# Expert blocks of a mixture of experts: rows loaded from a register address and turned on VectorE

## The chip, the cores and the metric

The kernel runs on one core of a Trainium2 chip. The metric is the device time of one execution in microseconds (us); a kernel's time is the median over several executions. All data are 32-bit floats.

## What is computed

The input is 8 images of 256 channels and 32 x 32 places, so 8 x 1024 tokens of width 256. Layer 0 is an attention with 8 heads, with its softmax over the queries, and a residual. Layer 1 is an attention without heads on the normalised tokens, a residual, a second normalisation, and a mixture of 8 experts of which each token uses two. The part that matters here is the mixture:

```python
logits = tokens @ router_w.T
probs = softmax(logits)
rw, re = top_k(probs, 2)
rw = rw / rw.sum(-1)
out = tokens
for e in range(8):
    h = gelu(tokens @ w1[e] + b1[e])
    y = h @ w2[e] + b2[e]
    out = out + combine[:, e:e+1] * y      # combine holds rw at re, else 0
```

w1 and w2 are 256 x 256 for each expert.

## The kernel before

The images are worked through one after the other. For each of the first seven, layer 0 (lines 437 to 642) and the attention of layer 1 (`attend`, line 645) run, then the tokens are routed: `dispatch` (line 849) computes for every token its two experts and a place within each expert, and GpSimd scatters the normalised rows into `rows`, a table in DRAM that has 7168 rows for each expert (line 917). The scatters are spread over layer 0 of the next image.

For the eighth image layer 0 runs, and with its products the expert stage `experts` (line 1018) works off the routed rows of the seven images. The rows of an expert are cut into blocks of 256 (`BR`); there are 63 block positions, and `plan` (line 926) computes on the chip which expert each block belongs to (`e_of`), at which row of `rows` it starts, and where its weights lie. It leaves two tables of integers: `row_at`, with one row number for each partition and block, and `w_at`, which points past the end of the table where a buffer already holds the right weights, so that nothing is loaded. After that, attention and a dense form of the experts run for the eighth image, with the results of the seven gathered and stored beside them.

One block goes through these steps:

- `fetch` (line 1024): GpSimd loads the weights of the block's expert from `wpack` into one of four buffers (`wb`, 128 partitions of 1282 values: w1 in two chunks of 128 input features, w2, b1, b2), then with a second indirect load 128 pieces of two neighbouring rows into `xr` (three buffers). TensorE turns them in four transposes of 128 x 128 into PSUM (`px`, line 1044), and VectorE copies them to `xb` (two buffers, line 1046), with features on partitions.
- `hidden` (line 1049): eight products into `ph` (line 1054), and two gelus on ScalarE (line 1064) into `hT`.
- `collect` (line 1073): eight products into `pe` (line 1079), the bias added by VectorE into `yb` (two buffers, line 1088), and a store to `y` from SP's queue (line 1093). A partition holds two neighbouring rows, 2 KB, and the store writes them in one piece.

The loop (line 1100) runs hidden of block b-1, fetch of block b, and collect of block b-2 in one turn. An engine issues its instructions in the order that a scheduler fixes when the program is built: it starts from the program text and moves an instruction ahead where its model sees the engine idle. `issue_after(ins)` holds a group of instructions behind `ins` on the same engine. A buffer's next load waits until its last reader is done: the weights of block b wait for pe and the bias addition of block b-4, which had that buffer.

After block 4 `places` (line 993) runs: for each of the seven images and each of the two choices, five small VectorE operations that turn a token's place within its expert into its row in `y` (`yat`). These are needed when the results are gathered (line 1163).

In layer 0 of every image but the first, SP also relays semaphores: `relay.nop()` (line 551) is an empty instruction on SP that waits for one half of the po products and that the other half waits for.

The squares that the change uses are in the kernel already in two places. `load_squares` and `residual` (lines 417 to 435) load the input so that VectorE's transpose, which turns each square of 32 x 32 for itself, gives the tokens on partitions; and `turn` (line 686) does the same with the attention weights, where 16 moves put the squares in their places.

Of the kernel before, what the change touches and what calls it, by code (L numbers as in the profile page):

```python
# [10 lines left out]
F32 = mybir.dt.float32  # L11
I32 = mybir.dt.int32
AF = mybir.ActivationFunctionType
ALU = mybir.AluOpType
# [5 lines left out]
def kernel(  # L20
# [23 lines left out]
    nc = tc.nc  # L44
    P = 128
    B, C, S = x.shape
    E, D, FF = w1.shape
# [3 lines left out]
    NCC = C // P  # L51
# [3 lines left out]
    NFC = FF // P  # L55
# [3 lines left out]
    WROW = NCC * FF + NFC * D + NFC + D  # L59
    NWB = 3  # L60
    NXB = NWB + 1

    dram = ctx.enter_context(tc.tile_pool(name="dram", bufs=1, space=bass.MemoryType.DRAM))
    const = ctx.enter_context(tc.tile_pool(name="const", bufs=1))
# [10 lines left out]
    def big(name):  # L75

        return ps_big.tile([P, 1024], F32, tag="big", name=name)
# [58 lines left out]
    for e in range(E):  # L136
# [12 lines left out]
    nc.gpsimd.iota(  # L149
        p_iota, [[1, 1]], base=0, channel_multiplier=1, allow_small_or_imprecise_dtypes=True  # L150
    )
    r_iota = const.tile([P, 1], F32, name="r_iota")
    nc.gpsimd.iota(
        r_iota, [[1, 1]], base=0, channel_multiplier=R, allow_small_or_imprecise_dtypes=True
    )
    ones = const.tile([P, P], F32, name="ones")
    nc.gpsimd.memset(ones, 1.0)

# [48 lines left out]


    NB = NT // NH2
    SQ = 32  # L210
    NQ = P // SQ

    def bcast(t, n):

# [66 lines left out]
    def pack():  # L281


        wp = wpack.rearrange("(e p) c -> e p c", p=P)
        for dc in range(NCC):
            nc.sync.dma_start(
                wp[:, :, ts(dc, FF)], w1.rearrange("e (dc p) f -> dc e p f", p=P)[dc]
            )
        at = NCC * FF
        for fc in range(NFC):  # L290
            nc.sync.dma_start(
                wp[:, :, at + fc * D : at + (fc + 1) * D],
                w2.rearrange("e (fc p) d -> fc e p d", p=P)[fc],
            )
# [142 lines left out]
    def layer0(b, xT, begun, routing, xs):  # L437
# [138 lines left out]
        for at in range(last + LAG + 1):  # L576
            g, j = steps[min(at, last)]

            early = at > LAG and j == 1 and (g, j) not in PROJECT
            if at <= last:  # L580
                with tc.issue_after(counted.ins) if counted else nullcontext():
                    score(at, 0, 0)
            if 0 < at <= last + 1:
                with tc.issue_after(counted.ins) if counted else nullcontext():
                    score(at - 1, 1, 1)
                second_max(at - 1, 1)
                soften(at - 1, 1)
            if at >= LAG:
                with tc.issue_after(counted.ins) if counted else nullcontext():
                    gather_values(at - LAG, 0)  # L590
                counted = None
            if at <= last:

                with tc.issue_after(seconds[1].ins) if 1 in seconds else nullcontext():
                    first_max(at, 0)
                score(at, 0, 1)
                score(at, 1, 0)
                second_max(at, 0)
                if not early:
                    soften(at, 0)  # L600
                with tc.issue_after(seconds[0].ins):
                    ahead = divide(at - 1) if at > 0 else seconds[0]
                with tc.issue_after(ahead.ins):
                    first_max(at, 1)
            elif at == last + 1:
                divide(last)
            if at == 0:
                begun.rest()
                share()
            if at >= LAG:  # L610
                array = gather_values(at - LAG, 1)
            if early:
                with tc.issue_after(copied[0].ins), tc.issue_after(copied[1].ins):
                    soften(at, 0)
            if at <= last and (g, j) in PROJECT:
                with tc.issue_after(firsts[at, 1].ins), tc.issue_after(array.ins):
                    share(firsts[at, 1])
                    pair, pq, mm = project_pair(b, xT, g + 1)
                qks.append(pair)
                if (g, j) == PROJECT[-1]:  # L620
                    with tc.issue_after(firsts[at, 1].ins):
                        t1 = residual(b, xs)
                if g == 0:
# [302 lines left out]
    def plan(group):  # L926
# [39 lines left out]
        )  # L966

        base = tmp("p_base", [E])
        nc.vector.tensor_scalar(base, first, -float(BR), r_iota, ALU.mult, ALU.add)
        work = tmp("p_work", [nb, E])  # L970
        lo, hi = tmp("p_lo", [nb]), tmp("p_hi", [nb])
        nc.vector.tensor_mul(work, mine, base.unsqueeze(1).to_broadcast([P, nb, E]))
        nc.vector.tensor_reduce(lo, work, AX.X, ALU.add)
        nc.vector.scalar_tensor_tensor(lo, b_iota[:, :nb], float(BR), lo, ALU.mult, ALU.add)
        nc.vector.tensor_scalar_min(lo, lo, float(cap - R))
        nc.vector.scalar_tensor_tensor(lo, e_of, float(cap), lo, ALU.mult, ALU.add)
        row_at = keep.tile([P, NBMAX], I32, tag="row_at", name=f"row_at_{n}", bufs=2)
        nc.vector.tensor_copy(row_at[:, :nb], lo)
# [14 lines left out]
    def places(group):  # L993

        first = group.first
        for b in group.items:
            gate, kept = group.kept[b]
            ats = []
            for k, (row, exp) in enumerate(kept):
# [13 lines left out]
                at = keep.tile([P, NT], I32, tag=f"yat{k}", name=f"yat{k}_{b}")  # L1013
                nc.vector.tensor_copy(at, to)
                ats.append(at)
            group.kept[b] = gate, ats

    def experts(group):
        n = group.n
        row_at, w_at = group.where  # L1020

        wbs_x = [*wbs, one.tile([P, WROW], F32, tag="v", name="wb_x")]

        def fetch(b):
            wb = wbs_x[b % NXB]
            nc.gpsimd.indirect_dma_start(
                out=wb[:, :],
                out_offset=None,
                in_=wpack[:, :],
                in_offset=bass.IndirectOffsetOnAxis(ap=w_at[:, b : b + 1], axis=0),  # L1030
                bounds_check=E * P - 1,
                oob_is_err=False,
            )
            xr = rowp.tile([P, R, D], F32, tag="xr", name=f"xr_{n}_{b}")
            nc.gpsimd.indirect_dma_start(
                out=xr.rearrange("p r d -> p (r d)"),
                out_offset=None,
                in_=group.rows[:, :],
                in_offset=bass.IndirectOffsetOnAxis(ap=row_at[:, b : b + 1], axis=0),
            )  # L1040
            px = big(f"px_{n}_{b}")
            for dc in range(NCC):
                for r in range(R):
                    nc.tensor.transpose(px[:, ts(dc * R + r, P)], xr[:, r, ts(dc, P)], ident)  # L1044
            xb = two.tile([P, NCC, BR], F32, tag="xb", name=f"xb_{n}_{b}")
            nc.vector.tensor_copy(xb.rearrange("p c t -> p (c t)"), px[:, : NCC * BR])
            return xb

        def hidden(b, xb):
            wb = wbs_x[b % NXB]  # L1050
            ph = big(f"ph_{n}_{b}")
            for fc in range(NFC):
                for dc in range(NCC):
                    nc.tensor.matmul(  # L1054
                        ph[:, ts(fc, BR)],
                        wb[:, dc * FF + fc * P : dc * FF + (fc + 1) * P],
                        xb[:, dc, :],
                        start=(dc == 0),
                        stop=(dc == NCC - 1),
                    )  # L1060
            hT = two.tile([P, NFC, BR], F32, tag=f"qk{b % 2}", name=f"hb_{n}_{b}")
            at = NCC * FF + NFC * D
            for fc in range(NFC):
# [4 lines left out]
                    bias=wb[:, at + fc : at + fc + 1],  # L1068
                    scale=1.0,
                )  # L1070
            return hT

        def collect(b, hT):
            wb = wbs_x[b % NXB]
            py = acc(f"pe_{n}_{b}")
            at = NCC * FF
            for r in range(R):
                for fc in range(NFC):
                    nc.tensor.matmul(  # L1079
                        py[:, ts(r, D)],  # L1080
                        hT[:, fc, ts(r, P)],
                        wb[:, at + fc * D : at + (fc + 1) * D],
                        start=(fc == 0),
                        stop=(fc == NFC - 1),
                    )
            at += NFC * D + NFC
            yb = two.tile([P, R, D], F32, tag="yb", name=f"yb_{n}_{b}")
            added = nc.vector.tensor_add(
# [1 line left out]
                py.rearrange("p (r d) -> p r d", d=D),  # L1090
                wb[:, at : at + D].unsqueeze(1).to_broadcast([P, R, D]),
            )
            nc.sync.dma_start(group.y[ts(b, BR), :].rearrange("(p r) d -> p r d", r=R), yb)
            if b == NXB:
                with tc.issue_after(added.ins):
                    places(group)


        rows, hiddens = {}, {}
        for b in range(group.nb + 2):  # L1100
            if b - 1 in rows:
                hiddens[b - 1] = hidden(b - 1, rows.pop(b - 1))
            if b < group.nb:
                rows[b] = fetch(b)
            if b - 2 in hiddens:
                collect(b - 2, hiddens.pop(b - 2))

    class Results:

# [235 lines left out]
    for b in range(B):  # L1345
# [6 lines left out]
        if b + 1 < B:  # L1352
# [3 lines left out]
            nc.sync.dma_start(groups[0].sums[b], t2)  # L1356
            routing = dispatch(b, n2, l, groups[0])
            continue
        experts(groups[0])
        others = Results(groups[0])  # L1360
        others.begin()
        norm = None
# [54 lines left out]
```

## Time and profile before

| | us |
|---|---|
| median of 3 runs | 2336.58 |
| the runs | 2336.16 to 2338.21 |
| profiled execution, its own time | 2335.55 |
| its span | 2333.5 |
| expert stage: first ph to end of last pe | 1877.51 to 2127.72 |

The granted clock of TensorE in the profiled execution is 0.995 of full speed. Engines that matter in the stage, from the timeline of an ordinary block, and the queues:

| What | Engine | Duration |
|---|---|---|
| ph, eight products | PE | 1.73 us in the chain |
| pe, eight products | PE | 1.73 us in the chain |
| px, four transposes | PE | 0.44 us in the chain |
| xb copy | DVE | median 691 ns |
| yb addition | DVE | median 691 ns |
| gelu, two a block | ACT | median 472 ns each |
| weights, issue of the load | POOL | median 1011 ns |
| rows, issue of the load | POOL | median 953 ns |
| y, issue of the store | SP's queue | median 320 ns |

PE is TensorE, PEld its weight loads, DVE VectorE, ACT ScalarE, POOL GpSimd, SP SyncE; SPq and ACTq are the instructions with which an engine starts a DMA. A name such as `xb<-px` says what an instruction writes and reads. In brackets stands how long the engine had been idle before it and what ended that. The chain of waits is followed back from the last instruction, so a piece in it is what the end waited for. The DMA share is the mean busy share of the core's 16 DMA engines.

### The profile page before, as it was taken

What the parts mean: (1) busy time and instruction counts of PE and PEld (TensorE: products, weight loads), DVE (VectorE), ACT (ScalarE), POOL (GpSimd) and SP (SyncE); (2) the same over time, 40 slices, a digit from 0 to 9 for tenths busy, and PEclk for the clock granted to TensorE, in tenths of its full rate; (3) what the DMA queues carried; (4) which work ended last, traced back from release to release, by engine and by line L of the source; (5) the groups of instructions that cost most, each with busy time, mean ns of one, the idle gap of its engine ahead of it and who ended that gap; (6) DMA issues with size and microseconds to landing.
All of it is one profiled execution on the core that took longest, in us unless ns stands there. A gap on an engine that the chain in (4) does not pass through costs nothing.

```text
span 2333.5 us, 37255 instructions
## 1 busy us (share of the span) xinstructions
PE 2297.1 (98%) x13375; PEld 1255.0 (54%) x13375; DVE 1513.0 (65%) x3660; ACT 1091.7 (47%) x1954; POOL 419.6 (18%) x391
## 2 busy tenths in 40 slices
PE   9999999999999999999999999999999999999898
PEld 3345534563456335633564356435553488887565
DVE  5775578557855785578647774777568763334865
ACT  3663366346634663556355645465545612222411
POOL 0000012000200030003000200020002234444663
PEclk9999999999999999999999999999999999999999
DMA  8995201020103010201020102000110256665664
GB/s 294 385 386 152 66 14 42 9 56 10 46 4 61 6 51 1 46 19 53 3 46 19 49 8 41 23 26 12 26 39 19 83 177 225 222 219 168 183 182 116
DMA packets 219232, 209.23 MB, mean 90 GB/s; under 512 B 120200, under 2 KB 162856, under 8 KB 217256
## 3 DMA queue, kind: packets, MB, share of 16 engines
q1 hardware_dynamic: 192952, 139.13, 19.8%
q0 software_dynamic: 25008, 67.20, 9.3%
q8 instruction: 107, 1.75, 0.3%
q10 hardware_dynamic: 1088, 0.52, 0.1%
q14 instruction: 77, 0.63, 0.1%
HBM read 108.88 MB, written 110.90 MB: 94 GB/s over the span
## 4 chain that ended last, share of the span: by engine, by line
PE 91%; DVE 4%; DMA 2%; issue 1%; ACT 1%; SPq 1%; POOL 0%; DVEq 0%; ACTq 0%; POOLq 0%
PE po L541 19%; PE psc L464 19%; PE ps L672 9%; PE py L713 8%; PE pqk L346 7%; PE pr L638 5%; PE pv L383 4%; PE ph L1054 4%; PE pe L1079 4%; PE pdy L1307 2%; PE pdh L1283 2%; PE px L657 2%; PE pqk L324 2%; PE px L1044 1%; DMA wb<-wpack,w_at 1%
## 5 line engine op out<-in xcount | busy, mean ns | idle before, releaser
L505 ACT ACTIVATE ex<-psc,nmax 128x1024 f32<-128x1024 f32 x512 | 570.1, 1114 | 304.4 <-DVE scrap L488 217.2
L464 PE MATMUL psc<-qk,qk 64*64 64x512 f32 x4096 | 576.9, 593 | 7.8 <-ACT ex L505 7.7
L541 PE MATMUL po<-ex,vs 64*64 64x512 f32 x4096 | 571.2, 592 | 1.2 <-DVE vs L521 0.3
L488 DVE TENSOR_SCALAR_CACHE_REDUCE scrap<-psc,nmax 128x512 f32<-128x512 f32 x512 | 384.3, 751 | 160.8 <-PE psc L464 134.7
L479 DVE TENSOR_REDUCE nmax<-psc 128x1 f32<-128x512 f32 x512 | 350.3, 684 | 9.5 <-PE psc L464 9.5
L464 PEld LDWEIGHTS psc<-qk,qk 64*64 64x64 f32 x4096 | 180.1, 132 | 284.2 <-ACT ex L505 135.8
L541 PEld LDWEIGHTS po<-ex,vs 64*64 64x64 f32 x4096 | 175.9, 132 | 273.7 <-issue 83.6
L713 PE MATMUL py<-n,aT 128*128 128x256 f32 x1024 | 231.4, 379 | 0.2 <-DMA aT<-sq 0.2
L672 PE MATMUL ps<-nT,xa 128*128 128x512 f32 x512 | 228.5, 592 | 0.0
L917 POOL DMA_INDIRECT rows<-n,d_at x112 | 108.8, 972 | 661.2 <-DVE nmax L479 658.4
L713 PEld LDWEIGHTS py<-n,aT 128*128 128x128 f32 x1024 | 193.9, 190 | 50.2 <-issue 23.3
L844 POOL TENSOR_TENSOR t<-t,n 128x2048 f32<-128x2048 f32 x8 | 36.2, 4531 | 874.7 <-DVE n L238 874.7
L697 ACT COPY aT<-sq 32x256 f32<-32x256 f32 x384 | 154.4, 402 | 72.8 <-DVE sq L690 41.3
L346 PE MATMUL pqk<-xT,wqkv 128*128 128x512 f32 x384 | 171.2, 599 | 0.0
L672 PEld LDWEIGHTS ps<-nT,xa 128*128 128x128 f32 x512 | 96.6, 190 | 102.4 <-issue 94.7
L680 DVE TENSOR_REDUCE nmax<-ps 128x1 f32<-128x1024 f32 x64 | 77.9, 1217 | 84.9 <-PE ps L672 84.9
L311 ACT ACTIVATE qk<-pqk,b_qks 128x512 f32<-128x512 f32 x124 | 85.6, 690 | 95.9 <-PE pqk L346 77.1
L346 PEld LDWEIGHTS pqk<-xT,wqkv 128*128 128x128 f32 x384 | 71.0, 190 | 99.9 <-issue 76.8
L383 PE MATMUL pv<-wqkv,xT 128*128 128x512 f32 x256 | 121.9, 605 | 2.1 <-ACT wqkv L106 1.1
L1163 POOL DMA_INDIRECT yk<-y,yat x112 | 110.3, 985 | 69.2 <-issue 26.2
L638 PE MATMUL pr<-wo,res 128*128 128x256 f32 x512 | 111.9, 379 | 0.3 <-ACT res L560 0.3
L1064 ACT ACTIVATE hb<-ph,wb 128x256 f32<-128x256 f32 x96 | 40.2, 470 | 144.8 <-issue 76.7
(191 smaller groups left out, 2441.1 us busy)
## 6 DMA issues: line engine op xcount, KB each, us to landing
rows<-wb SPq DMA_DIRECT2D x7, 8192.0 KB
y<-yb SPq DMA_DIRECT2D x63, 256.0 KB
aT<-sq SPq DMA_DIRECT2D x384, 32.0 KB
xs<-in_x_dram SPq DMA_DIRECT2D x64, 128.0 KB
out_dram<-oT SPq DMA_DIRECT2D x60, 128.0 KB
xT<-in_x_dram SPq DMA_DIRECT2D x7, 1024.0 KB
sums<-t SPq DMA_DIRECT2D x7, 1024.0 KB
o<-sums SPq DMA_DIRECT2D x7, 1024.0 KB
```

The costliest lines, as they stand in the source:

```text
L346: mm = nc.tensor.matmul(pq[:, ts(n, 512)], wqkv[:, cc, t, ts(g, P)], xT[:, cc, ts(n, 512)], start=(cc == 0), stop=(cc == NCC - 1),)
L383: nc.tensor.matmul(pv, self.xT[:, cc, ts(i, P)], wqkv[:, cc, 2, :], start=(cc == 0), stop=(cc == NCC - 1),)
L464: mm = nc.tensor.matmul(pss[at, h][ts(c, DK), ts(n, 512)], k[r, j * P + c * DK : j * P + (c + 1) * DK], q[r, ts(n, 512)], start=True, stop ...
L479: firsts[at, h] = nc.vector.tensor_reduce(nmax, pss[at, h][:, ts(0, 512)], AX.X, ALU.max, negate=True)
L488: seconds[h] = nc.vector.tensor_scalar(scrap, pss[at, h][:, ts(1, 512)], -1.0, nmaxes[at, h], ALU.mult, ALU.min, accum_out=nmax,)
L505: nc.scalar.activation(ex, pss.pop((at, h)), AF.Exp, bias=nmaxes.pop((at, h)), scale=1.0, accum_out=sums[at][:, h : h + 1],)
L541: mm = nc.tensor.matmul(po[n][ts(h, DK), :], vss[at][keys, h, :], exps[at, h][keys, ts(n, 512)], start=(j == 0 and turn == 0), stop=(j == ...
L638: nc.tensor.matmul(pr[:, :C], res[:, g, ts(i, P)], wo[:, g, :], start=(g == 0), stop=(g == NPAIR - 1))
L672: nc.tensor.matmul(psc[:, ts(n, 512)], xa[:, ec, ts(i, P)], nT[:, ec, ts(n, 512)], start=(ec == 0), stop=(ec == NCC - 1),)
L697: move(to[ts(k, SQ), a], since[ts(a, SQ), k])
L713: nc.tensor.matmul(py[:, :D], aT[m], n1[:, m, :], start=(m == 0), stop=(m == NT - 1))
L1163: ins = nc.gpsimd.indirect_dma_start(out=self.slot(at)[:, k, :], out_offset=None, in_=self.group.y[:, :], in_offset=bass.IndirectOffsetOnAxis(
```

## The change

- **Rows.** `plan` leaves in `row_at` the block's first row instead of one row number for each partition. `fetch` reads that number into a register of SP (`value_load`), and SP loads the block in four transfers to 32 partitions each: partition 32k + t gets, for each of the eight runs of 32 tokens, the 64 features of quarter k of token t, in pieces of 256 bytes.
- **Turning.** `turned` is one VectorE transpose in squares of 32 x 32 from `xr` to `xb`, with no TensorE transposes and no PSUM in between. It is held behind the last `divide` of layer 0. Features thus lie in another order on the partitions, and `pack` writes w1 into `wpack` in that order, in eight copies instead of two.
- **Order.** The loop turns once more: hidden of block b-2, the loads of block b, the turning of block b-1, collect of block b-3. The products pe are held behind the last ph of the following block.
- **y.** Tokens lie in their own order, so a partition holds rows p and 128 + p, and the store writes pieces of 1 KB. It is issued from ScalarE instead of SP.
- **places** becomes a generator, and one of its 14 pieces runs behind the yb of each block from block 4 on.

```diff
+    SQ = 32
+    NQ = P // SQ
+    DQ = D // NQ
+    RUN = BR // SQ
...
         wp = wpack.rearrange("(e p) c -> e p c", p=P)
-        for dc in range(NCC):
-            nc.sync.dma_start(
-                wp[:, :, ts(dc, FF)], w1.rearrange("e (dc p) f -> dc e p f", p=P)[dc]
-            )
+        src = w1.rearrange("e (k cc c) f -> k cc e c f", k=NQ, c=SQ)
+        for k in range(NQ):
+            for cc in range(NCC):
+                nc.sync.dma_start(wp[:, ts(k, SQ), ts(cc, FF)], src[k, cc])
...
             elif at == last + 1:
-                divide(last)
+                evicted["divided"] = divide(last)
...
-        nc.vector.tensor_scalar(base, first, -float(BR), r_iota, ALU.mult, ALU.add)
+        nc.vector.tensor_scalar_mul(base, first, -float(BR))
...
-        nc.vector.tensor_scalar_min(lo, lo, float(cap - R))
+        nc.vector.tensor_scalar_min(lo, lo, float(cap - BR))
...
-            group.kept[b] = gate, ats
+                if k > 0:
+                    group.kept[b] = gate, ats
+                yield
...
-            xr = rowp.tile([P, R, D], F32, tag="xr", name=f"xr_{n}_{b}")
-            nc.gpsimd.indirect_dma_start(
-                out=xr.rearrange("p r d -> p (r d)"),
-                out_offset=None,
-                in_=group.rows[:, :],
-                in_offset=bass.IndirectOffsetOnAxis(ap=row_at[:, b : b + 1], axis=0),
-            )
-            px = big(f"px_{n}_{b}")
-            for dc in range(NCC):
-                for r in range(R):
-                    nc.tensor.transpose(px[:, ts(dc * R + r, P)], xr[:, r, ts(dc, P)], ident)
+            xr = rowp.tile([P, RUN, DQ], F32, tag="xr", name=f"xr_{n}_{b}")
+            with tc.issue_after(loads[-1].ins) if loads else nullcontext():
+                at = nc.sync.value_load(
+                    row_at[0:1, b : b + 1], min_val=0, max_val=E * group.cap - BR
+                )
+            mine = group.rows[bass.ds(at, BR), :].rearrange("(s t) (k d) -> k t s d", s=RUN, k=NQ)
+            for k in range(NQ):
+                loads.append(nc.sync.dma_start(xr[ts(k, SQ)], mine[k]))
+            return xr
+
+        def turned(b, xr):
             xb = two.tile([P, NCC, BR], F32, tag="xb", name=f"xb_{n}_{b}")
-            nc.vector.tensor_copy(xb.rearrange("p c t -> p (c t)"), px[:, : NCC * BR])
+            with tc.issue_after(behind.ins):
+                nc.vector.transpose(
+                    xb.rearrange("p cc (s t) -> p s cc t", t=SQ),
+                    xr.rearrange("p s (cc c) -> p s cc c", c=SQ),
+                )
             return xb
...
+            with tc.issue_after(last.ins):
+                for r in range(R):
+                    for fc in range(NFC):
+                        nc.tensor.matmul(
+                            py[:, ts(r, D)],
...
-            nc.sync.dma_start(group.y[ts(b, BR), :].rearrange("(p r) d -> p r d", r=R), yb)
-            if b == NXB:
+            nc.scalar.dma_start(group.y[ts(b, BR), :].rearrange("(r p) d -> p r d", r=R), yb)
+            if b >= NXB:
                 with tc.issue_after(added.ins):
-                    places(group)
+                    next(placed, None)
...
         rows, hiddens = {}, {}
-        for b in range(group.nb + 2):
-            if b - 1 in rows:
-                hiddens[b - 1] = hidden(b - 1, rows.pop(b - 1))
+        placed = places(group)
+        assert group.nb - NXB >= 2 * len(group.items)
+        last = None
+        for b in range(group.nb + 3):
+            if b - 2 in rows:
+                hiddens[b - 2], last = hidden(b - 2, rows.pop(b - 2))
             if b < group.nb:
                 rows[b] = fetch(b)
-            if b - 2 in hiddens:
-                collect(b - 2, hiddens.pop(b - 2))
+            if b - 1 in rows:
+                rows[b - 1] = turned(b - 1, rows.pop(b - 1))
+            if b - 3 in hiddens:
+                collect(b - 3, hiddens.pop(b - 3), last)
```

More of the change, by code (lines that the diff above doesn't have):

```diff
@@ L151 @@
     )
-    r_iota = const.tile([P, 1], F32, name="r_iota")
-    nc.gpsimd.iota(
-        r_iota, [[1, 1]], base=0, channel_multiplier=R, allow_small_or_imprecise_dtypes=True
-    )
     ones = const.tile([P, P], F32, name="ones")
@@ L209 @@
     NB = NT // NH2
-    SQ = 32
-    NQ = P // SQ
     def bcast(t, n):
@@ L1015, in places, with experts @@
                 ats.append(at)
-            group.kept[b] = gate, ats
-    def experts(group):
+                if k > 0:
+                    group.kept[b] = gate, ats
+                yield
+    def experts(group, behind):
         n = group.n
         row_at, w_at = group.where
+        loads = []
         wbs_x = [*wbs, one.tile([P, WROW], F32, tag="v", name="wb_x")]
@@ L1033, in fetch @@
             )
-            xr = rowp.tile([P, R, D], F32, tag="xr", name=f"xr_{n}_{b}")
-            nc.gpsimd.indirect_dma_start(
-                out=xr.rearrange("p r d -> p (r d)"),
-                out_offset=None,
-                in_=group.rows[:, :],
-                in_offset=bass.IndirectOffsetOnAxis(ap=row_at[:, b : b + 1], axis=0),
-            )
-            px = big(f"px_{n}_{b}")
-            for dc in range(NCC):
-                for r in range(R):
-                    nc.tensor.transpose(px[:, ts(dc * R + r, P)], xr[:, r, ts(dc, P)], ident)
-            xb = two.tile([P, NCC, BR], F32, tag="xb", name=f"xb_{n}_{b}")
-            nc.vector.tensor_copy(xb.rearrange("p c t -> p (c t)"), px[:, : NCC * BR])
+            xr = rowp.tile([P, RUN, DQ], F32, tag="xr", name=f"xr_{n}_{b}")
[8 more added lines that the diff above has]
+        def turned(b, xr):
+            xb = two.tile([P, NCC, BR], F32, tag="xb", name=f"xb_{n}_{b}")
+            with tc.issue_after(behind.ins):
[3 more added lines that the diff above has]
+                )
             return xb
@@ L1053, in hidden @@
                 for dc in range(NCC):
-                    nc.tensor.matmul(
+                    last = nc.tensor.matmul(
                         ph[:, ts(fc, BR)],
@@ L1070, in hidden, with collect @@
                 )
-            return hT
-        def collect(b, hT):
+            return hT, last
+        def collect(b, hT, last):
             wb = wbs_x[b % NXB]
@@ L1076, in collect @@
             at = NCC * FF
[L1077 to L1085, printed above, removed]
+            with tc.issue_after(last.ins):
[3 more added lines that the diff above has]
+                            py[:, ts(r, D)],
+                            hT[:, fc, ts(r, P)],
+                            wb[:, at + fc * D : at + (fc + 1) * D],
+                            start=(fc == 0),
+                            stop=(fc == NFC - 1),
+                        )
             at += NFC * D + NFC
@@ L1358 @@
             continue
-        experts(groups[0])
+        experts(groups[0], evicted["divided"])
         others = Results(groups[0])
```

## The prediction

> **What bounds the kernel now.** I read the busy table first, then the chain of waits, then the timeline of one expert block, then the chain and the stage windows around a change of expert.
>
> From the page, TensorE is busy almost all the span and is 91% of the chain that ended last:
>
> ```profile
> PE 2297.1 (98%) x13375; PEld 1255.0 (54%) x13375; DVE 1513.0 (65%) x3660; ACT 1091.7 (47%) x1954; POOL 419.6 (18%) x391
> PE 91%; DVE 4%; DMA 2%; issue 1%; ACT 1%; SPq 1%; POOL 0%; DVEq 0%; ACTq 0%; POOLq 0%
> ```
>
> So an instruction taken off TensorE is a gain as long as nothing else becomes late. The expert stage starts with the first ph at 1877.51 us and ends with the last pe at 2127.72: 250.2 us for 63 blocks. One block in the timeline (start, duration, engine, line):
>
> ```profile
> 1925.80 0.57 PEld L1044 LDWEIGHTS px<-ident,xr 128*128 128x128 f32 x4
> 1925.93 1.01 POOL L1026 DMA_INDIRECT wb<-wpack,w_at  x1 [1.63 <-issue]
> 1926.45 1.89 PE L1079 MATMUL pe<-wb_x,hb 128*128 128x256 f32 x8
> 1926.65 0.69 DVE L1046 COPY xb<-px 128x512 f32<-128x512 f32 x1 [1.47 <-PE px L1044]
> 1927.25 0.95 POOL L1035 DMA_INDIRECT xr<-rows,row_at  x1 [0.30 <-issue]
> 1928.17 1.89 PE L1054 MATMUL ph<-xb,wb 128*128 128x256 f32 x8
> 1928.38 0.69 DVE L1088 TENSOR_TENSOR yb<-pe,wb_x 128x512 f32<-128x512 f32 x1 [1.04 <-PE pe L1079]
> ```
>
> In the chain the eight ph and the eight pe of a block take 1.73 each and the four px transposes 0.44, so a block lasts 3.89 with no gap. The reader is to see that VectorE, ScalarE and GpSimd are idle for more than half of it. Where the expert changes, new weights come in, and one load of the group is late:
>
> ```profile
> 1930.50 1.59 PE pe L1079 x8
> 1932.09 1.43 issue
> 1933.53 0.18 issue
> 1933.72 6.57 DMA wb<-wpack,w_at
> 1940.42 1.97 PE ph L1054 x8
> ```
>
> The load goes out at 1933.72; the ph before it starts at 1935.96 in the chain, so this one was due 3.89 later, at 1939.85, and starts at 1940.42. So a load has 6.13 us from its issue, and this one takes 6.6. Windows show how full the DMA engines are (length, busy of each engine, granted clock, DMA share, GB/s):
>
> ```profile
> 10.00:11.00 1.00, 0.35 (x3) 0.37 (x4) 0.50 (x2) 0.00 (x0) 0.00 (x0) 1.00 0.83 188
> 1660.00:1690.00 30.00, 30.00 (x110) 20.59 (x109) 16.23 (x29) 20.37 (x47) 0.00 (x0) 1.00 0.27 41
> 1694.00:1700.00 6.00, 6.00 (x30) 4.58 (x29) 3.01 (x5) 1.05 (x1) 0.00 (x0) 1.00 0.98 178
> 1935.50:1947.18 11.68, 11.28 (x58) 9.64 (x58) 3.88 (x6) 2.50 (x6) 5.41 (x6) 1.00 0.90 280
> 1951.07:1962.75 11.68, 11.68 (x61) 10.29 (x60) 4.15 (x7) 2.52 (x7) 5.89 (x6) 1.00 0.40 135
> 2059.00:2067.00 8.00, 8.00 (x42) 6.87 (x41) 2.76 (x4) 1.68 (x4) 4.13 (x5) 1.00 0.88 295
> ```
>
> Between changes of expert the share is 0.40; in the four blocks after one it is 0.88 to 0.90. Block by block over the stage there are seven such groups, 28 loads. That is the second resource near its end, and the change asks more of it.
>
> **px leaves TensorE.** 63 blocks times 0.44; two of them ran before 1877.51, so 61 x 0.436 = 26.6 us off the stage. What is left is 3.46 a block.
>
> **xb on VectorE.** A 128x512 transpose in squares instead of the 0.69 copy from PSUM. The residual's transpose of 128x1024 (L430) has a median of 1.218, so half, 0.61. With yb's 0.69 and a piece of places (five operations, 0.2 us each, 1.1) VectorE has 2.4 in 3.46: hidden, and a lateness of up to one block is covered, since the transpose runs one block before its ph. Without that cover it would cost 0.61 + the load's landing once, not per block. The start wins something: today ph of block 1 waits for px and xb and starts 0.77 late; then it has nothing to wait for. -0.8.
>
> **places in pieces.** Today all 14 run behind block 4's yb and hold xb back; TensorE waits 0.6 + 0.5 + 0.2 for them (L1011, L1007, L1001). -1.3.
>
> **pe behind the next ph.** The order today is ph, px, pe of the block before; it stays so without px. 0. ScalarE's two gelus (0.84) have 3.46 to run in.
>
> **y stored from ScalarE.** One issue of 256 pieces: the output's on ScalarE's queue cost 0.44 each. It waits for yb, 0.9 after pe's end, with the next block's gelus queued behind it; these are wanted 1.7 after pe's end at the earliest and have 2.5 to spare after that. 0; if ScalarE were late by more, pe would wait.
>
> **x loads.** GpSimd loses 0.95 a block (not on the path). SP gains a register load and four issues of 256 pieces. Such an issue took 0.608 in aT (median), 0.31 at least in xs, and 0.83 at the start of the kernel with the engines full (8 in 6.68). A register load stands in no row: at least SP's 0.04 between two issues, at most the 2.1 us of the shortest GpSimd load; I take one issue's 0.6, as it moves four bytes. 4 x 0.608 + 0.6 = 3.0 of 3.46; bounds 1.3 and 5.4. Hidden at 3.0, since xr has three buffers. SP also relays layer 0's semaphores; the program text puts the loads behind these. If the scheduler moves three blocks' loads among them, up to 3 x 3.0 = 9 us; I take 0, as x isn't wanted before 1877 and landings of 4 us are the norm. The packing of w1 in eight copies instead of two lies beside layer 0 of the first image, where SP relays nothing: 0.
>
> **The DMA engines** are where I expect the gain to be eaten. Per block and all 16 engines: x and y together now 0.40 x 3.89 = 1.56, or 0.78 each; a weight load (0.89 - 0.40) x 3.89 = 1.91. New x: 256 KB in 1024 pieces of 256 B, four transfers to 32 partitions each. Not in the trace; the nearest rows: xs (DRAM to 32 partitions, 512 B pieces, the third window) 178 GB/s at 0.98, so 182, gives 1.44 us; b_v (256 B pieces, 128 partitions, first window) 188 at 0.83 gives 1.16; aT (128 B, 32 partitions, on chip, second window) 41 at 0.27 gives 1.72. Bounds: 0.78 (as now) and 2.88 (xs's rate counted in pieces, 1024 of them). I take xs, 1.44. New y: 1 KB pieces for 2 KB; between 0.78 and xs's 1.44; 0.85. A block with a weight load then needs 1.91 + 1.44 + 0.85 = 4.20 against 3.46: 0.74 short, x 28 = 20.7 us if all of it is paid. Blocks without need 2.3: no loss.
>
> The page "DMA: Bandwidth & Descriptors" of the Trainium skill (Why small descriptors are slow) puts three cycles on each piece beside one per 32 bytes, so two pieces of 256 B take 22 where one of 512 takes 19. By it xs's 1.44 would become an estimated 1.67 and the forecast some 3 us later. No row here shows 256 B pieces to 32 partitions, so it is neither borne out nor denied.
>
> **The weights' time budget.** From pe of block b-4 to ph of block b lie two blocks, before and after. So it shrinks with the block, by 2 x 0.436 = 0.87, from 6.13 to 5.26. Seven late loads later by 0.87: 6.1 us, the lower end, if the DMA engines serve no worse. The upper end is the 20.7 less the 3.5 of lateness at changes of expert that is there now (250.2 less 63 x 3.46 less 26.6 is 5.6 of gaps, less 0.8 and 1.3): 17.2. Below zero I exclude: nothing makes a load shorter by 0.87. Since x may run ahead by three buffers part of the shortage is deferred; I take the middle, +11.7.
>
> **Sum.** 2333.5 - 26.6 - 0.8 - 1.3 + 11.7 = 2316.5 of span; around the span lie 2.05 (2335.55 timed in the profiled run), and the median shown, 2336.58, is 1.0 above that run: 2319.6, so **2319**.
>
> **Rivals.** (1) *All hidden*: x and y defer so far that weights are no later than now: 2333.5 - 28.7 + 3.1 = 2308. For it: 0.40 outside the groups leaves room. Against: 0.89 inside, and a shorter budget. (2) *SP becomes the bound*: with the issues at 0.83 as under full engines and the register load at 0.55, 3.87 a block, 63 x 3.87 = 243.8 for 250.2, so 2330; slower from 3.97. For it: eight issues took 6.68 at the start. Against: only 0.5 each at 1693. (3) *Slower side: x's small pieces make the DMA engines the bound.* Place: the 28 blocks with weights. 28 x (2.76 + x) + 35 x 3.46 passes 250.2 at x = 1.85 us. At 2.3, midway between aT and the piece count, it gives 262.8, so 2349; at 2.88 also the other blocks exceed 3.46 and it ends near 2375. For it: xs is slow per piece already. Against: b_v and aT move smaller pieces faster.
>
> **Chances.** Forecast 0.52 (own range 2311 to 2327), all hidden 0.16, SP 0.12, DMA 0.20. What this kernel's measurement can tell from no change is about 0.2%, 4.7 us. Faster by more: 0.50 + 0.16 + 0.05 of SP's = 0.71; within: 0.02 + 0.03 = 0.05; slower: 0.04 + 0.20 = 0.24. The range goes to 2306, leaving out a part of "all hidden" (0.06), and to 2348, leaving out the dearer half of DMA (0.12).
>
> **What would show it.** No px of line 1044's kind; a block of 3.46 between changes of expert; xb as a transpose near 0.61; TensorE waiting on wb at changes of expert by 1 to 3 us a group, with a DMA share near 1. SP issues of x under 3.46 us a block mean SP is off the path; blocks longer than 3.46 between changes of expert, with TensorE waiting on xb or x, make the forecast wrong, by SP if its issues follow without a pause, by the DMA engines if the share is near 1 there.

## The result, and the profile after

| | us |
|---|---|
| before, median of 4 runs (2336.16 to 2338.21) | 2337.05 |
| after, median of 4 runs (2418.26 to 2421.05) | 2419.88 |
| after over before, with its 95% interval | 1.0354 (1.0336 to 1.0372) |
| span of the profiled execution, before and after | 2333.53 and 2415.37 |
| expert stage, first pr to the next attention's first pt_n: before | 1863.43 to 2127.56: 264.1 |
| expert stage: after | 1870.46 to 2210.53: 340.1 |

The change makes the kernel 3.5% slower; the forecast was 2319. Of the 81.8 us that the span grew by, 75.9 lie in the expert stage and 7.0 ahead of it. What follows it got shorter by 1.1. The pr products, which close layer 0, run just ahead of the blocks; pt_n is the first product after them.

The page after, busy time and the chain that ended last:

```profile
PE 2289.5 (95%) x13123; PEld 1226.8 (51%) x13123; DVE 1512.4 (63%) x3660; ACT 1092.9 (45%) x1955; POOL 358.7 (15%) x327
PE 79%; SPq 8%; DVE 5%; DMA 4%; issue 2%; ACT 1%; POOL 0%; DVEq 0%; ACTq 0%; POOLq 0%
```

TensorE's busy time is only 7.6 us below that of before, though px is gone, and it is no longer busy nearly throughout: 95% for 98%, and 79% of the chain for 91%. VectorE's busy time is that of before (1513.0), so VectorE has not become the bound by its amount of work. An ordinary block in the timeline (start, duration, engine, line; in brackets the idle time ahead of it and what ended that):

```profile
2075.82 0.69 DVE L1094 TENSOR_TENSOR yb<-pe,wb_x 128x512 f32<-128x512 f32 x1 [3.81 <-PE pe L1085]
2076.43 0.70 DVE L1048 STREAM_TRANSPOSE xb<-xr 128x512 f32<-128x512 f32 x1
2077.18 1.99 PE L1059 MATMUL ph<-xb,wb 128*128 128x256 f32 x8 [1.40 <-DVE xb L1048]
2079.01 1.89 PE L1085 MATMUL pe<-wb,hb 128*128 128x256 f32 x8
2080.94 0.69 DVE L1094 TENSOR_TENSOR yb<-pe,wb 128x512 f32<-128x512 f32 x1 [3.81 <-PE pe L1085]
2081.55 0.70 DVE L1048 STREAM_TRANSPOSE xb<-xr 128x512 f32<-128x512 f32 x1
```

The reader is to see a ring. VectorE sits idle for 3.81 us until pe is done, adds yb, and only then turns the rows that the very next ph needs. So a block is ph, then pe, then yb, then xb, one after the other: from 2075.82 to 2080.94 it is 5.12 us, for 3.46 forecast. While places runs, its five operations stand between yb and xb, and the period is 6.28 (ph at 1915.95 and 1922.23). The waits between 1870 and 2212 (engine, instruction and what it waited for: us in all, times, longest) show how much that is in all:

```profile
PEld ph L1059 <- DVE xb L1048: 111.8, 55, 3.0
PE ph L1059 <- DVE xb L1048: 89.8, 55, 2.6
```

The weights of ph are loaded beside its products, so the two lines are not to be added. Between 1877 and 2128 before, this wait was:

```profile
PE ph L1054 <- DVE xb L1046: 0.8, 1, 0.8
```

TensorE thus waits 89.8 us for xb. The stage grew by less, since the 27 us of px left it. And the order was not so from the start. Earlier in the same stage, with the same instructions:

```profile
1892.78 0.71 DVE L1048 STREAM_TRANSPOSE xb<-xr 128x512 f32<-128x512 f32 x1 [0.88 <-PE ph L1059]
1894.30 1.89 PE L1059 MATMUL ph<-xb,wb 128*128 128x256 f32 x8
1894.50 0.69 DVE L1094 TENSOR_TENSOR yb<-pe,wb 128x512 f32<-128x512 f32 x1 [1.02 <-PE pe L1085]
1896.03 1.89 PE L1085 MATMUL pe<-wb_x,hb 128*128 128x256 f32 x8
1896.23 0.71 DVE L1048 STREAM_TRANSPOSE xb<-xr 128x512 f32<-128x512 f32 x1 [1.03 <-PE ph L1059]
1897.76 0.59 PE L1059 MATMUL ph<-xb,wb 128*128 128x256 f32 x2
```

Here xb runs while pe runs, ahead of that pe's addition, and ph follows ph after 3.46. In the trace VectorE's instructions follow each other as xb 4, yb 1, xb 5, yb 2, xb 6, yb 3, yb 4, xb 7, yb 5, yb 6, xb 8, yb 7, xb 9, and so on: from block 8 the turning of block b stands behind the addition of block b-2, where the program text has it ahead of that addition. VectorE works in order, and pe of block b-2 is held behind ph of block b-1. These two together close the ring.

### The profile page after: what moved, and what is told of

It reads as the page before. It is cut to its first block, busy times and chain, and to the rows that moved or that the text cites. A ratio compares the mean times of both kernels' runs of the same rounds, so it can differ in the third digit from the quotient of the medians.

```text
span 2415.4 us, 37653 instructions
## 1 busy us (share of the span) xinstructions
PE 2289.5 (95%) x13123; PEld 1226.8 (51%) x13123; DVE 1512.4 (63%) x3660; ACT 1092.9 (45%) x1955; POOL 358.7 (15%) x327
## 4 chain that ended last, share of the span: by engine, by line
PE 79%; SPq 8%; DVE 5%; DMA 4%; issue 2%; ACT 1%; POOL 0%; DVEq 0%; ACTq 0%; POOLq 0%
PE po L539 16%; PE psc L462 15%; PE py L711 8%; PE ps L670 8%; PE pqk L344 6%; SPq L268 5%; PE ph L1059 4%; PE pr L636 4%; PE pv L381 4%; PE pe L1085 3%; PE pdh L1294 2%; PE pdy L1318 2%; PE px L655 2%; PE pqk L322 2%; SPq L286 1%
## 5 line engine op out<-in xcount | busy, mean ns | idle before, releaser
L1059 PE MATMUL ph<-xb,wb 128*128 128x256 f32 x384 | 100.1, 405 | 69.6 <-DVE xb L1048 68.1
L1094 DVE TENSOR_TENSOR yb<-pe,wb 128x512 f32<-128x512 f32 x48 | 33.2, 691 | 169.0 <-PE pe L1085 160.4
L1059 PEld LDWEIGHTS ph<-xb,wb 128*128 128x128 f32 x384 | 72.6, 198 | 96.9 <-DVE xb L1048 85.0
```

The lines of the kernel that those rows point to most:

```text
L1059: last = nc.tensor.matmul(ph[:, ts(fc, BR)], wb[:, dc * FF + fc * P : dc * FF + (fc + 1) * P], xb[:, dc, :], start=(dc == 0), stop=(dc == ...
```

## The experiments

Three theories to start with. **A**: the place of xb behind yb on VectorE costs the 76 us. **B**: the x loads are late, held up on SP by y stores or by their own price. **C**: both share it. e1 to e4 ran on one chip, e5 to e8 on a second and e9 to e11 on a third, and times are set against the kernel before on the same chip. On the second the kernel before took 2361.65, and each kernel that was traced there 227 to 232 us from pt_n to the end, for 205 to 212 elsewhere; why was not settled. So the stage from pr to pt_n is what is compared:

| run | median us (runs) | before beside it | stage us |
|---|---|---|---|
| after | 2419.88 (4) | 2337.05 | 340.1 |
| e1_order | 2344.03 (10) | 2338.26 | 259.8 |
| e2_order_ypool | 2336.82 (1) | 2338.26 | 254.9 |
| e3_nohold | 2481.11 (1) | 2338.26 | 401.1 |
| e4_ysp | 2419.81 (1) | 2338.26 | 343.8 |
| e5_order_noreload | 2330.46 (1) | 2361.65 | 229.3 |
| e6_early_order | 2363.16 (1) | 2361.65 | 259.7 |
| e7_order_ypool_late | 2350.03 (5) | 2361.65 | 251.4 |
| e8_order_ypool_noreload | 2330.20 (1) | 2361.65 | 229.3 |
| e9_order_nohold | 2360.03 (1) | 2338.34 | 275.9 |
| e10_ypool_late_xwide | 2338.61 (1) | 2338.34 | 255.0 |
| e11_ypool_late_again | 2335.09 (10) | 2338.34 | 253.2 |

**e1_order: the turning put ahead of the addition.** The addition is held behind the newest transpose; nothing else changes.

```diff
-                nc.vector.transpose(
+                turns.append(nc.vector.transpose(
...
-            added = nc.vector.tensor_add(
+            with tc.issue_after(turns[-1].ins):
+                added = nc.vector.tensor_add(
```

> VectorE's order alone is changed: each yb is held behind the next turning xb, so that xb of block b-1 stands ahead of yb of block b-3 all through the stage. Theory A (the order yb, then xb on VectorE closes a chain ph, pe, yb, xb, ph of 1.6 + 2.1 + 0.6 + 0.75 = 5.1 us a block): the block falls to 3.46 us between changes of expert, TensorE waits for weights only, and the time is 2310 to 2335. Theory B (SP's loads of x are late: the profile has SP waiting 147 us for y's landings): the block stays above 4.7 us, xb now waits for xr, and the time is 2395 or more. Theory C (both: with the order mended the x loads, which wait for a y store's semaphore, are next): a block of about 4.5 us and 2370 to 2390.

Measured: 2344.03, or 1.0022 of before (1.0012 to 1.0032). That is 76 of the 83 us lost, by one pair of instructions on VectorE. It is above A's interval and far below the others': the place of xb is the cause of the loss, but not of all that the forecast missed. Of the waits of ph these are left:

```profile
PE ph L1059 <- DVE xb L1048: 17.9, 12, 3.0
PE ph L1059 <- DMA wb<-wpack,w_at: 2.9, 3, 2.0
```

So theory A's "for weights only" did not hold. Windows of e1_order (length; busy of PE, PEld, DVE, ACT, POOL; clock; DMA share; GB/s) over a change of expert, then between changes:

```profile
1934.28:1949.20 14.92, 12.36 (x50) 10.07 (x48) 6.82 (x21) 2.52 (x6) 3.00 (x3) 0.89 0.93 274
1952.65:1966.47 13.82, 13.82 (x66) 12.16 (x65) 7.44 (x18) 3.35 (x8) 3.99 (x4) 1.00 0.52 141
```

Between changes four blocks take 13.82, 3.46 each, with TensorE busy without a gap. Over a change TensorE idles 2.6 of 14.9 us with the DMA share at 0.93 and a granted clock of 0.89. What the stage of e1_order still loses lies there. That stage is 4.3 us shorter than before; the span is longer all the same, as pr starts 8.3 later (1871.75) and what follows the stage takes 212.2 for 206.0.

**e2_order_ypool: and y stored from GpSimd.** In e1_order SP's x loads still wait for y stores to land (58.6 us in 44 waits, 147.4 in 58 in the changed kernel), though they share no data. In the trace the transfers that SP and ScalarE start in the stage share eight completion semaphores, each used 36 or 37 times, so that an x load can have to wait for the y store that used its semaphore before it.

```diff
-            nc.scalar.dma_start(group.y[ts(b, BR), :].rearrange("(r p) d -> p r d", r=R), yb)
+            nc.gpsimd.dma_start(group.y[ts(b, BR), :].rearrange("(r p) d -> p r d", r=R), yb)
```

> As the kernel with VectorE's order mended, and y is stored from GpSimd, so that no load of x can wait for a y store by a shared semaphore. Theory A: within 5 us of the kernel with the order alone. Theories B and C: faster than that by 30 us or more, as the x loads can run ahead.

Measured: 2336.82 in a single run, 7 below e1_order, with 5.0 in the stage: the stage is at the edge of theory A's 5 us, the total just beyond it, and both are far from the 30 of B and C. The waits of ph for the rows are gone but for 1.5 us; those for the weights are 13.5. All waits of ph in the stage fell only from 20.8 to 18.2; the rest of the 5.0 is TensorE's busy time, 236.5 for 239.1, with a granted clock of 0.99 for 0.98. So taking y's stores off the semaphores of x is worth about 5 us, as far as nothing else in the move to GpSimd counts.

**e3_nohold and e9_order_nohold: pe not held behind the next ph**, in the changed kernel and in e1_order.

```diff
-            with tc.issue_after(last.ins):
+            with nullcontext():
```

> The changed kernel with pe not held behind the next ph; everything else as changed. The scheduler then puts pe of a block straight behind its own ph, and xb of the next behind yb of this one. Theory A: the chain grows by the gelus, about 1 us, to 5.9 to 6.1 us a block, and the time to 2455 to 2480. Theory B: x sets the pace, so no change, 2410 to 2430.

> e1_order without the hold: the transpose stands ahead of the older addition, and the down matmuls of a block aren't held behind the next block's up matmuls, so that they come right behind their own up matmuls. Theory A (the hold is worth the gelu's tail, which e3_nohold shows as 0.61 us of TensorE's waiting in a block, and no more; the transpose's order alone is worth the rest): 39 us above e1_order for 64 blocks, less what the slower blocks give back at the changes of expert; 2360 to 2385 beside a kernel before of 2338, with the waits of the down matmuls for the gelu at 30 to 40 us and next to none of the up matmuls for the transpose between the changes. Theory B (without the hold the order is worth nothing, since the addition still ends last in each block): 2440 to 2481.

Measured: 2481.11 and 2360.03. In the waits of e3_nohold, then of e9_order_nohold:

```profile
PE ph L1059 <- DVE xb L1048: 87.2, 54, 2.6
PE pe L1085 <- ACT hb L1069: 33.1, 54, 0.6
```

```profile
PE pe L1085 <- ACT hb L1069: 33.1, 54, 0.6
PE ph L1059 <- DVE xb L1048: 0.4, 1, 0.4
```

Both wait 0.6 for the gelu in each block, which the hold hides; only the first waits for xb. Both total times came as theory A of each had them, if just above e3's upper end and at e9's lower end. The stage makes a table of two by two: xb behind yb, 340.1 with the hold and 401.1 without; xb ahead, 259.8 and 275.9. So the hold is worth having, by 16 us where the order is right, and it did not cause the loss. Of the 61 us that it is worth in the wrong order only half are waits (120.3 for 89.8); the rest is TensorE's busy time in the stage, 280.7 for 250.3, with a granted clock of 0.91 for 0.98.

**e4_ysp: y stored from SP as before, the order left as the change has it.**

```diff
-            nc.scalar.dma_start(group.y[ts(b, BR), :].rearrange("(r p) d -> p r d", r=R), yb)
+            nc.sync.dma_start(group.y[ts(b, BR), :].rearrange("(r p) d -> p r d", r=R), yb)
```

> The changed kernel with y stored from SP again; VectorE's order stays yb, then xb. Theory A: the same chain, a block of 5.1 us or a little more where x comes later, 2415 to 2435. Theory B: the x loads stand behind each y store in SP's queue and its wait for yb, so the block grows by 1 us or more, 2470 or more.

Measured: 2419.81, the time of the changed kernel, with a stage 3.7 longer. Where y is stored from moves next to nothing while the ring sets the period.

**e5_order_noreload and e8_order_ypool_noreload: e1_order and e2_order_ypool with weights loaded for four blocks only.**

```diff
-            nc.gpsimd.indirect_dma_start(
+            if b < NXB:
+                nc.gpsimd.indirect_dma_start(
```

> The transpose stands ahead of the older addition, as in e1_order (2344.0), and the experts' weights are gathered for the first four blocks only: the later blocks use those four buffers, so the weights of blocks 4 and on are left out of the computation. Theory A (what e1_order still loses is the 28 gathers of weights at the 7 changes of expert, on DMA engines that its rows take to 0.9 and more there): 2311 to 2320, some 26 us below e1_order, with no wait of the up matmuls for the weights and next to none for the transposed rows. Theory B (the rest is the x loads held up behind the landing y stores, whatever the weights do): 2338 to 2346, with the transposed rows waited for as before, 17.9 us in all.

> e2_order_ypool (2336.8) with the experts' weights gathered for the first four blocks only; the weights of blocks 4 and on are left out of the computation. Theory A (its remaining loss over the all-hidden 2308 is the gathers of weights): 2308 to 2316. Theory B (the loss lies in the places or at the start): 2328 to 2337.

Measured: stages of 229.3 in both, 30.5 and 25.6 below their pairs. The times themselves, 2330.46 and 2330.20, missed theory A's intervals, and the second fell into theory B's; but the intervals were set for a kernel before of 2338. To the kernel before on their chip both stand as 0.987, which beside 2338 would be some 2307. The only wait of ph's products in e5_order_noreload, which lies ahead of pr, and a window:

```profile
PE ph L1060 <- issue: 1.5, 1, 1.5
```

```profile
1920.00:1954.50 34.50, 34.50 (x161) 30.38 (x160) 21.53 (x61) 8.40 (x20) 0.00 (x0) 1.00 0.56 153
```

TensorE is busy for every one of ten blocks of 3.45, and in neither of the two kernels does ph wait for weights or rows. So all that is left in e1_order and e2_order_ypool over the whole of the stage is due to the weight loads, and the x loads make ph wait in e1_order only beside them. With the 28 loads went the 31 issues on GpSimd that load nothing; the two were not tried apart.

**e6_early_order: e1_order with the x loads a turn earlier.**

```diff
-                rows[b] = fetch(b)
+                fetch(b)
+            for ahead in ([0, 1] if b == 0 else [b + 1]):
+                if ahead < group.nb:
+                    rows[ahead] = fetch_x(ahead)
```

> e1_order with each block's four x loads issued one turn earlier, two blocks ahead of the up matmuls that take their transpose. Theory A (the DMA engines' bandwidth at the changes of expert is the limit): within 5 us of e1_order, 2339 to 2349, as the same bytes cross the same engines, and the wait only moves from the transposed rows to the weights. Theory B (the x loads are late because of the y stores ahead of them, and one block, 3.46 us, of lead covers the longest such wait): 2320 to 2332, with the waits for the transposed rows under 5 us in all.

Measured: a stage of 259.7, for 259.8. Theory A's time, but not its path: ph still waits for the rows (20.7 us), and SP for landing y stores (56.7). A place further ahead in the program is no use to a load that waits for the store whose semaphore it takes over.

**e7_order_ypool_late and e11_ypool_late_again: what the runs point to.** y is stored from GpSimd behind the next weight load (`put`, called in `fetch`, issues what `collect` left in `stores`), and the first ph runs behind the last pr; the transpose stands ahead of the addition as in e1_order.

```diff
+            put(loaded)
...
-            nc.scalar.dma_start(group.y[ts(b, BR), :].rearrange("(r p) d -> p r d", r=R), yb)
+            stores.append((b, yb))
...
+                with tc.issue_after(evicted["projected"].ins):
+                    hiddens[b - 2], last = hidden(b - 2, rows.pop(b - 2))
```

> Three edits on the changed kernel: the transpose ahead of the older addition; y stored from GpSimd, issued behind the next block's gather of weights; the first up matmuls behind the last of the projection matmuls ahead of the stage. Theory A (against 2336.8 with y ahead of the weights' gather in e2_order_ypool: the gathers go out 0.6 us sooner, which at 7 changes of expert is 4 us, and the start gives back up to 3.5): 2327 to 2333, faster than the kernel before by 0.2 to 0.4 per cent. Theory B (the full DMA engines set the end at the changes, whoever issues first): 2334 to 2339, no different from the kernel before.

> e7_order_ypool_late once more, on whatever chip this call gets. Theory A (its gain lies in the expert stage, which the chip does not change): 0.993 to 0.997 of the kernel before, the stage in 250 to 253. Theory B (the gain was that chip's): 0.998 to 1.002.

Measured: 0.9949 of the kernel before (0.9936 to 0.9963), more than e7's theory A had, and on another chip 0.9989 (0.9979 to 0.9998). The stage is 251.4 and 253.2, so it is 11 to 13 us under the 264.1 of before on both (before was traced on one chip alone), while the total gave 11.6 us on the one and 3.3 on the other: e11's theory A holds for the stage to 0.2 and fails for the total, which fell into theory B's interval. The three edits were not tried apart. In e11's trace 4.3 us are lost ahead of the stage (pr starts at 1867.7 for 1863.4), and the attention after it waits 2.2 for copies that stand behind the last additions. This version is faster than both kernels, than the kernel before by 0.5% on one chip and 0.1% on the other.

**e10_ypool_late_xwide: x in pieces of 2 KB.**

```diff
-            mine = group.rows[bass.ds(at, BR), :].rearrange("(s t) (k d) -> k t s d", s=RUN, k=NQ)
+            mine = group.rows[bass.ds(at, BR), :].rearrange("(k t s) d -> k t (s d)", k=NQ, t=SQ)
```

> e7_order_ypool_late (0.9949 of the kernel before; 251.4 us from the first pr to the next attention's first pt_n) with each x load reading 2 KB in one piece for each partition in place of eight pieces of 256 bytes; which element of the rows goes where is left out, the bytes are the same. Theory A (what the DMA engines lack at the changes of expert is what the small pieces cost): the stage in 243 to 248, the up matmuls' waits for weights at most half of the 13.6 us. Theory B (the pieces cost next to nothing, the weights' own bytes fill the engines): the stage in 250 to 252.5, the waits at 12 to 14.

Measured: a stage of 255.0, nothing won; it is even above theory B's interval. Window 1882 to 2000 of e10_ypool_late_xwide, then of e11_ypool_late_again:

```profile
1882.00:2000.00 118.00, 111.80 (x508) 95.06 (x506) 60.96 (x150) 27.41 (x64) 51.57 (x57) 1.00 0.70 215
```

```profile
1882.00:2000.00 118.00, 111.04 (x501) 93.69 (x501) 58.08 (x144) 28.20 (x66) 52.87 (x59) 1.00 0.82 222
```

The DMA share falls from 0.82 to 0.70 and the waits for weights stay: 15.1 us for 15.2. So the small pieces cost the DMA engines 0.12 of their time here and the kernel nothing that shows. In the chains of both kernels a weight load lasts 5.45 to 7.64 us from its issue, for the 5.26 of the prediction's budget. In e11 the loads are issued late as well: yb has two buffers, and additions wait for y stores to land:

```profile
DVE yb L1096 <- DMA y<-yb: 77.5, 28, 4.6
```

A block's addition reads the bias from its weight buffer, so the next load into that buffer waits for it. In e11's chain over the stage landing y stores are 22% and weight loads 20%; in e10's they are 5.5% and 23.6%. Over a change of expert the engines moved 278 GB/s in e10 and 279 in e11, and 280 before; what holds them there is open.

## Why the prediction was wrong

- **The step that failed** is "xb on VectorE … VectorE has 2.4 in 3.46: hidden, and a lateness of up to one block is covered, since the transpose runs one block before its ph". The work is near what was costed: 0.70 for the 0.61, and VectorE is busy for 105 of the stage's 340 us. But the cover was taken from the program text, and the built order on VectorE does not have it: xb of block b stands behind yb of block b-2. The step on **pe behind the next ph** ("0") belongs to it. The hold makes yb later by one ph; that is harmless by itself, and worth 16 us, but it is what xb behind yb then waits for. Together +76 in e1_order against the changed kernel, where the prediction had 0. That a scheduler fixes each engine's order and moves instructions from the text's was known beforehand, and no rival was made of it.
- **px, places and the start in the stage** were right. e5_order_noreload shows the stage without late weights: 34.8 below before. Predicted were 26.6 + 0.8 + 1.3, with the 3.5 of lateness that before had at changes of expert 32.2, and ten of ph's first sixteen products (2.2) had moved ahead of pr: 34.4. The 26.6 took px of two blocks to lie ahead of the stage; the trace of before has one there (four transposes between 1859.67 and 1863), so it is 27.0, and the lateness 3.1.
- **The DMA engines**: the weight loads at the changes of expert were the right second place, and were sized at half. The prediction gives the weights 11.7, and 3.5 that was there before: 15.2, at most 20.7. Measured: 30.5 with y on ScalarE, 25.6 with y on GpSimd. Two of its inputs did not hold. The price of x's pieces, at the centre of its working, decided nothing in e10. And the shorter time budget, counted once in each group of four loads, falls due on several: e11 has 21 late loads at 7 changes. Some 5 us of the 30.5 came through the semaphores that x loads share with y stores (e2).
- **x loads on SP** cost less than thought: the register load is 0.27 + 0.15 us for the 0.6 taken, and an issue has a median of 0.317 for 0.608. The page "DMA: Bandwidth & Descriptors" of the Trainium skill (Latency and other measured facts) has a floor of about 600 ns for such a load. The 63 here had 263 ns at least and 488 at most. SP was not the bound, as rival 2 would have had it, but it waited for y.
- **SP's relays**, taken at 0 with an upper end of 9 us, cost something. In the changed kernel, just when the x loads go out:

```profile
1840.62 28.35 SPq L1042 DMA_DIRECT2D xr<-rows  x16
1841.94 0.21 PEld L539 LDWEIGHTS po<-ex,vs 64*64 64x64 f32 x8 [3.20 <-SPq L549]
1841.94 1.09 PE L539 MATMUL po<-ex,vs 64*64 64x512 f32 x8 [2.32 <-SPq L549]
```

  TensorE waits 2.32 us for a relay that SP issues beside the loads. The start as a whole lost: pr begins 7.0 later, of which 2.2 are the ten products of ph ahead of it and 1.5 an idle stretch before them.
- **y from ScalarE** at 0 was right as far as the queue of ScalarE goes (e4 is no faster), and wrong in what it does to SP's loads (e2).
- **The rivals.** Rival 3 came nearest in time (2375) and for another reason: blocks were longer also between changes of expert, but with a DMA share of 0.35 there. The sign that was to show the forecast wrong, such blocks with TensorE waiting on xb, came, but it went with neither of the two causes named for it. None of the three rivals named the mechanism that decided. Had the order been as in the text, the kernel would have come at e1_order's 2344: inside the range, at its slow end, and 0.2% slower than before, not faster. Its span is 27.3 above the 2316.5 of the forecast: 12.7 in the stage, where the weights cost 15.3 more than forecast; 8.3 ahead of the stage, for which the prediction took 0; and 6.2 behind it, which it does not mention.

Why the scheduler puts xb behind yb here was not settled. In the traces it does so with y on SP as well (e4_ysp).

## What to carry to other kernels

An instruction on an engine that works in order costs what stands ahead of it, not its duration: for each one that is moved, write down its neighbours in the built order and follow the ring through them, since a cover of one block in the text is gone with one exchanged pair. A hold on one engine, right by itself, moves the work that follows it on another; look at what is queued behind that. And an earlier load helps only where nothing it waits for, a shared semaphore too, comes as late as before.

## What the runs showed of the hardware

The granted clock of TensorE fell in the changed kernel where the idle gaps were longest. Three ph of the places stretch, and two windows, of the changed kernel:

```profile
1915.95 1.99 PE L1059 MATMUL ph<-xb,wb 128*128 128x256 f32 x8 [2.55 <-DVE xb L1048]
...
1922.23 3.47 PE L1059 MATMUL ph<-xb,wb 128*128 128x256 f32 x8 [2.55 <-DVE xb L1048]
...
1929.98 1.99 PE L1059 MATMUL ph<-xb,wb_x 128*128 128x256 f32 x8 [2.56 <-DVE xb L1048]
```

```profile
1920.00:1925.00 5.00, 2.77 (x7) 2.24 (x8) 2.03 (x7) 0.00 (x0) 1.00 (x1) 0.68 0.40 107
2020.83:2031.00 10.17, 7.44 (x32) 5.91 (x32) 2.59 (x4) 1.68 (x4) 2.00 (x2) 1.00 0.35 94
```

The same eight products after the same gap of 2.55 us take 1.99 or 3.47; the slow ones come at 1922, and again in windows near 1942, 1963 and 1983. Later, with gaps of 1.40 in each 5.12, the clock stayed at 1.00. The page "TensorE: Matmul & The Clock Gate" of the Trainium skill (Part 1) puts the fall at a whole idle window of some 3.4 us. Here gaps of 2.55 in a period of 6.28 were enough about every third time. So a stall somewhere between 1.4 and 2.55 us a block began to cost more than itself: some 1.5 us, four times. The period differs with the gap, so these runs do not tell which of the two decides. In e3_nohold, where each block of the places stretch adds a gap of 0.61 to the one of 2.55, the clock stayed down for most of it:

```profile
1920.00:2012.00 92.00, 62.09 (x155) 41.50 (x154) 22.16 (x65) 7.54 (x18) 9.60 (x10) 0.63 0.30 84
```
